# Spreading the gates of a dense expert layer from SBUF instead of DRAM, with all x tiles loaded first and a new order of streams

## The chip, the cores and the metric

One core of one Trainium2 chip runs the whole kernel. The metric is the device time of one execution in microseconds (us). Its engines are TensorE (PE, with its weight loads as PEld), VectorE (DVE), ScalarE (ACT), GpSimd (POOL) and SyncE (SP, which issues most DMAs here); sixteen DMA engines move the data. [...]

## The reference

The input is x with 8 images of 512 tokens and 128 features. Four layers are added to it one after the other, each on a layer norm of the running x:

```python
x = x + attention(layernorm(x))        # causal softmax attention, one head of 128
x = x + experts(layernorm(x))          # f = 0
x = x + rwkv_block(layernorm(x))       # a time mix with a scan over 512 tokens, and a channel mix
x = x + experts(layernorm(x))          # f = 1
```

The expert layer has 32 experts with hidden size 64. Each token takes the four experts with the highest softmax scores, and its gate for an expert is that score; an expert takes at most 2048 tokens. On top stands one shared expert of hidden size 128:

```python
y[tok] += (silu(xg @ W1[e]) * (xg @ W3[e])) @ W2[e] * gate      # for each expert e and its tokens
out = y + (silu(x @ Ws1) * (x @ Ws3)) @ Ws2
```

All is in float32.

## The kernel before, in words

**Streams.** The work is written as Python generators, each of which stands for one image or one page group and yields after every few instructions. A string `ORDER` of 2257 two-character entries says which generator goes on next. The instructions of each engine and each queue stand in exactly that order; nothing is reordered later. The streams are:

- `a0` to `a7`: `attention(b)` for image b, up to and with the routing of the first expert layer (`route`).
- `r0` to `r7`: `rwkv(b)`, up to and with the routing of the second.
- `x` and `y`: the shared expert of the first and the second expert layer.
- `s` and `t`: `scatter`, 16 indirect DMAs by which POOL writes the tokens of an image to pages of single experts in DRAM (`xs`).
- `k l m n` and `K L M N`: the four stages of `experts`, by page group: `turned` (load xg from xs, transpose), `up` (first product, acl, and gates), `down` (transposed back, hz), `give` (second product o, store of oc to `ys`). One group has up to 20 units of four pages.
- `u` and `v`: `combine`, 16 indirect DMAs that add rows of `ys` to `res`.
- `d` and `D`: `full_up`, and `e` and `E`: `full_down`, for images that use no pages.

**Two ways through the experts.** `RUNS` says that in the first layer images 0 and 7, and in the second images 6 and 7, go through all 32 experts densely, and the others through pages. Lower-case letters belong to the first layer, capitals to the second; so D6 and D7 are the two dense images at the end.

**The dense way.** `route` ends in `gates`, which makes the gate of every token and expert, transposes it to 32 partitions (one an expert) by 512 tokens, and copies it from PSUM to the SBUF tile gT (L493). That tile goes to a DRAM tile gd (L495). `full_up` then runs over 16 pairs of experts. For pair i a DMA on SP's queue fills the tile g of 128 partitions: row 2i of the gates 64 times, then row 2i+1 64 times (L692). PE multiplies the image (fT) by the pair's two weight blocks (ac, L703), ACT takes a tanh (fh, L706), and VectorE forms the activation (L709), multiplies g by the second product (L710) and both together (L711). `full_down` multiplies the result by the pair's second weights and sums over all pairs in one PSUM tile (fsum, L677), which is copied to `res` (L724) and, in the second layer, stored.

**Buffers of g.** There are four. Three loads are issued at the start of a stream, and pair i issues the load of pair i+3 ahead of its own products:

```python
        for i in range(3):
            load(i)
        yield
        for i in range(NP):
            load(i + 3)
```

The tile gT comes from the pool `work`, of which 26 buffers go round among many uses.

**The start.** SP issues, in this order: the x tiles of images 0 to 3, the clearing of the first page group's xs with zeros (two DMAs of 2.6 MB) and a strip of ys, the x tiles of images 4 to 7, and the expert weights (pair, w2s, w13s). The small weights go on ACT's queue. The clearing of the second page group follows inside `attention(0)`.

Of the kernel before, what the change touches and what calls it, by code (L numbers as in the profile page):

```python
# [79 lines left out]


ORDER = (
    "a2a0a2a1a0a2a2a0a1a3z0a2a0a1a6a3z0a0a2a3a4a2a0a1a0a6a6a4a1a2a2a5a0z0a0a2a2a1a4a5a0a0a2a5a2a0a0a2"
    "a1a3a0a3a2a7a2a0a2a0a2a1a2a2a0a3a7a0a2a1a6a3a0a0a7a2a0a2a1a2a1a0a2a1a2a2a3a0a2a1a4a3a1a2a2a0a0a1"
    "a2a0a0a3a2a0a5a1a2a2a3a2a0a0a1a1a3a2a1a1a3a0a1a2a0a7a3a0a2a0a1a2a0a3a2a0a1a3a2a6a1a0a3a1a6a0a3a6"
    "a2a1a0a3a6a2a2a0a1a0a3a2a6a2a2a0a1a6a6a0a1a3a0a1a1a0a3a0a1a6a0a1a1a0a0a3a6a3a3a1a1a3a0a6a6a1a0a0"
    "a3a1a6a2a1a3a0a6a2a3a6a4a3a4a3a4a1a1a3a4a4a1a0a5a4a4a5a1a1a3a0a6a3a1a0a3a1a6a1a4a6a3a4a4a1a3a6a1"
    "a5a3a6a3a4d0a6a5a1a3a3a6a1a1a3a2a1a4a2a5a4a4a5d0a2a1d0a5a5a2a5x0x0a2a1a2s1a3a3a6x2a4a5a6x2x0x2x2"
    "a5a6a3a4a3x2x2a6s2a4a4d0a3x2a6a3a4a6a5x0a3a4a6a5a4s2a3a6a4x0a6a3a3a4a5d0a3d0s2x0a3a6x0a7a3a6l0a6"
    "a4a7s3l0a6l0a6a4a5d0a4a5a4x3a6a4a6x3d0s3a4d0a4a5d0a7a5a5a7a5a7a4a5a7d0a6a4a5x3s3a6a4a5a4x3a5a4a5"  # L90
    "x3a4a5x3a4a5s3a5x3a5a5a7a5e0a7a5a7e0a7a5d0a4e0a5d0a7e0s2a5a6a4a5d0a5d0a6a7a6e0d0a6a7a5a7x1a5s1d0"
    "a7x1x1a4a7e0a7a4d0a4d0a4a7a4a7a7x1s1a4d0d0a7d0e0d0a7a4x1s1d0d0d0a4a4d0a7e0a4e0x1k0a5d0a6a4a5a6x1"
    "d0a5d0k0a4a5k0e0a5d0s4k0l0k0x4l0l0a5d0x4d0a5l0s4d0m0a5e0m0l0a5d0d0e0l0l0l0s4m0a5m0k0k0k0l0k0d0a5"
    "n0s4n0l0a5d0l0l0d0n0m0d0n0e0m0k0l0k0a7s5n0l0l0l0l0n0a6a7l0l0x4l0k0a6m0k0k0a6e0s5k0m0m0x5m0l0a6x5"
    "n0d0n0d0n0l0l0x5s5a6x5l0n0a7x4a7a6k0l1m0k0x5l1m0x5d0s6l1l0x5x4n0l0l0l0l0n0k0l0l0m0l0k0a7m0k0l0a7"
    "k0s6m0l0l0n0l0m0a7n0k0l0a7k0m0l0l0n0l0m0x4n0s6a7k0x4l0k0m0l0l0n0l0m0a7n0n0a7k0l0n0s6k0m0l0l0a7l0"
    "m0k0l0a7k0a7m0n0m0x6n0l0s5l0n0l0x6l0n0k0l0l0m0x6x6k0l0m0e0k0l0x6k0a7m0l0l0n0l0m0x6n0a7a7k0l0k0m0"
    "l0n0l0l0a7m0l0n0a7k0x6l0m0k0k0n0k0l0a7l0m0l0n0a7k0a7m0k0n0m0n0n0l0a7l0l0n0k1l0a7a7m0a7l0l0a7m0n0"
    "l0l0n0k1l0l0m0l0a7k1m0k1l1a7k1m0l1l1n0l1m0x7n0l1x7m1x7k1l1l1l1n0k1x7n0m1m1k1x7m1l1k1n1l1l1l1l1n1"
    "u2k1m1l1l1l1k1n1m1x7n1m1l1x7m1k1l1l1n1l1k1e7n1l1u2m1l1l1k1l1n1m1k1d0n1d0m1k1d0m1n1k1l1n1n1l1l1d7"  # L100
    "l1l1u2n1k1m1l1l1l1k1e0m1k1m1l1k1m1n1l1l1l1l1n1k1m1l1l1l1k1n1u2m1k1m1n1l1m1k1n1l1l1d0l1n1d0m1d0k1"
    "m1n1k1l1n1n1u1l1l1l1l1n1k1m1l1l1l1k1e0m1k1m1r2e0l1m1k1n1r0d7n1r2d7n1l1l1l1r0n1k1m1r2k1r0u1r0d7l1"
    "m1r0l1n1r0d7e7l1r0l1n1r2u1m1k1r0r0m1k1l1d7r0r0d7r0l1l1l1l1r0u1n1r0m1k1n1l1r2e7r2r0r2r0r0r0r0r0m1"
    "u3r0l1n1k1d7r0n1r0r2k1d7r2k1r0k1r2r0u3r0r0l1r0m1r1m1n1r0l1n1k1r1l1l1l1r0m1r1r0r1u3r2r2d7r1l1r1e7"
    "l1r0r1r0m1u3r0d7r0l1r1r0r2l1d7r1r0r2r2r2r2r0r1m1r0r0r1r1d7r0r0m1r3r1l1r0r0l1r1r3l1n1r0l1r0r1n1r3"
    "r1r1r3m1r0r0m1r1r1r1r2r1n1r0r2r3d7r0e7r0r1n1n1r1d7n1r0r0r1r0r1r0u4r0r0r1r1r0r1r0r1r2r0r1r0u4r0r0"
    "r1r2r1r0y0r1r3t0r2r1r3r2y0r1r1r3r2r3r1t0r2r1r3r1r1r3r3r2r1r1d7r3r2r1t0r3r1r3r2y0d7r1r2r1r3r3d7t0"
    "r3d7r3e7r1r1r3r3r2d7r1r2u4r3r2r1e7r2d7r3y0r2r2r2r3r2r2r1r2r2r3u4r2r2r1r2r2r3r3r1d7r3r1r3r2d7r1u5"
    "d7r1y0r2d7r1r4d7r1d7e7r4r1r2d7r3r2u5r1r4r4r1r4r1d7r2e7d7e7r4r4r1r3r2r3u5r1y1r4r4d7y1r3r4r4d7y1r3"
    "d7r3r4r2d7y1u5r4r3r4r4r4r4d7r3r4r3y1r4r4y1r3r4d7r3y1u6e7r4r3r4r3e7r3r3r4y0r3r4r3y0r5u6r4r4r2r2r3"  # L110
    "d7r3r4r4r5r2r3d7r2r3r4d7r2u6e7r5r2r5r4r2r5r2r5d7d7r4r5r3r2r2d7r2u6r4r5e7r5r4r4r2r4r5r5r5r2r4L0r3"
    "r3d7t2r4L0d7r4L0r6r5r4d7r3r5r4r4d7d7r5r6r4r4t2r3r6e7r5r5r4r4r5r5r5r5r6r5r3t2r6r5e7r4r3r4d7r5r5t2"
    "y2r4r4y2r5r5r6r3r4r6r5t1r4r5r6r6r4r3d7r6r6r4r3r3e7r4r5r4e7t1r4r6r5r5r4r5r6r5r6r4r3r6t1r4r3r5r5r6"
    "r5r4r5r5r5t1r4r5r5r5r5r5r5r6r4r4r6t4y4r5r6r5r6y4K0r6r6r5r5K0t4K0K0K0L0r6L0L0L0L0K0M0L0L0L0M0N0t4"
    "K0r6M0N0K0L0M0N0K0r6N0L0L0L0L0t4K0M0L0L0L0M0N0K0r6M0N0K0L0M0r3N0K0L0L0r7y3N0r5r6y3r5t3r5L0L0y3M0"
    "L0L0K0y4M0r5L0K0N0r5r6y2M0N0K0r6t3r5M0L0K0N0r5r5y3N0y4r5L0L0L0r6y3M0K0r5r5t3M0L0K0N0y3N0r5y2y3r7"
    "r5L0r6r5y5L0r6L0L0t5K0M0L0K0L1r7M0L1y4N0L0L1y2r7L0L0r6K0L0N0M0t5r6r7r7r6r6M0r7K0L0t5L0N0r6r7K0N0"
    "M0L0K0M0r6L0L0N0L0r6L0N0M0t5L0L0K0L0r6M0N0K0L0r6M0N0L0K0M0r6N0L0L0K0t3N0L0r6M0L0K0r6M0N0L0L0K0N0"
    "L0r6M0L0K0r6M0L0L0K0y5y5N0r6M0N0L0M0K0L0N0L0L0K0r6N0M0L0r6M0r6K0N0K0K0N0L0r6r7L0L0K0L0r7r6r7r6M0"
    "K0L0r7M0N0L0L0K0L0N0r6r7L0M0L0K1r7y5M0L0y4r6r7N0r7r7M0y4L0N0y5M0r6L0N0L0L0r6K1r7y5N0K1r6r7M0L1y5"  # L120
    "M0K1N0L1L1r6L1K1N0r7M1L1r6r6M1N1r6r7K1N1v0y2L1L1r6K1L1L1y2r6L1L1r7M1L1r6K1y6M1N1K1r7y6M1L1M1v2N1"
    "N1L1L1y6K1L1N1y6K1L1D6y6M1L1L1K1r7y6M1K1L1L1y6N1L1L1r7v2M1N1K1E6M1N1L1K1L1N1M1r7K1M1r7K1L1L1L1L1"
    "r7N1v2L1L1r7M1N1K1M1L1N1K1L1N1M1L1L1K1M1L1N1K1M1L1N1M1r7N1L1L1L1v2K1N1D6K1r7D6M1D6r7K1L1M1N1L1L1"
    "L1K1D6N1D6v0M1K1D6M1r7N1K1L1N1r7D6L1L1r7v2D6r7L1K1D6r7M1r7v0M1L1K1r7N1L1L1D6L1N1K1M1K1r7M1E6r7L1"
    "v0N1D6L1L1D6r7N1E6r7r7L1L1r7M1L1K1M1r7L1L1K1v1M1L1v0r7M1N1L1L1L1K1N1N1K1L1N1M1L1L1K1L1r7v1M1K1M1"
    "L1r7M1r7N1K1N1N1L1L1L1K1K1D6N1r7K1D6M1r7v1r7E6D6E6L1M1N1L1L1L1L1N1r7M1L1L1L1E6M1N1r7M1D6v1N1M1D6"
    "N1D6r7N1r7D6r7D6E6D6r7v4D6r7r7v1r7D6r7E6D6r7r7y7y7D6y7v4D6D6y7E6D6y7D6D6y7E6y7v4D6D6D6E7E6D6D6D6"
# [15 lines left out]
def kernel(ctx: ExitStack, tc: tile.TileContext, x, small, vecs, w13, w2, out):  # L143
    nc = tc.nc
# [536 lines left out]
    def full_up(f, b):  # L683

        n = f"{f}_{b}"
        _, gd, xT, _ = routed[f][b]
        loaded = {}

        def load(i):
            if i < NP:  # L690
# [1 line left out]
                nc.sync.dma_start(  # L692
                    out=loaded[i], in_=gd[2 * i : 2 * i + 2].unsqueeze(1).to_broadcast([2, H, S])
                )
# [319 lines left out]
```

## Time and profile before

| | us |
|---|---|
| Runs shown | median 1059.47, from 1058.66 to 1060.27 |
| The profiled execution, in all | 1047.35 |
| Its span, first to last instruction | 1045.6 |
| PE busy | 806.6 (77% of the span) |
| POOL busy | 617.1 (59%) |
| VectorE busy | 588.2 (56%) |
| ScalarE busy | 474.1 (45%) |
| g loads (L692) | 64, of 256 KB each |
| gd stores (L495) | 4, of 64 KB each |
| Data moved by DMA | 108.15 MB, 103 GB/s on average |

Busy shares are averages over stages with different limits; no engine is busy all the time. So the lines to look at are those of waits and of the chain of work that ended last. A line such as `958.40 17.41 DMA g<-gd` in the chain gives the start, the length and what was waited for. A line of the timeline gives the start, the length, the engine, the line of the kernel, the operation, what it writes and reads, their shapes, and in brackets how long the engine stood idle before it and what ended that. In a DMA view, the share of a queue is the time of its packets as a share of sixteen engines over the stretch that is asked for.

### The profile page before, as it was taken

Reading aid. Unit: us, or ns where it says so; the run is one execution under the profiler, and the core shown is the slowest. Engines: PE = TensorE matmul, PEld = TensorE weight load, DVE = VectorE, ACT = ScalarE, POOL = GpSimd, SP = SyncE. Lnnn points to the kernel's source line nnn. Section 1 sums busy time; section 2 is a strip of 40 time slices with the busy share of each in tenths; the row PEclk is TensorE's granted clock in tenths of the full one; section 3 lists DMA queues with packets and bytes.
Section 4 is the critical chain, followed back from the end, with each engine's and each line's share of the span. In section 5 each row is a group of like instructions: output and inputs, shape, how many; then the busy total and the mean of one; then the engine's idle time right before and its main releaser. Section 6 shows DMA issues by size and latency. Waiting matters only on the chain.

```text
span 1045.6 us, 14396 instructions
## 1 busy us (share of the span) xinstructions
PE 806.6 (77%) x4096; PEld 559.8 (54%) x4096; DVE 588.2 (56%) x2008; ACT 474.1 (45%) x1130; POOL 617.1 (59%) x682
## 2 busy tenths in 40 slices
PE   4488689777599668787889888786993989856664
PEld 2266356555498555453455545564783757534332
DVE  2457576655245436699779679662482445522332
ACT  4375243323276447473445555455672656201010
POOL 4200778555701828848888888878036685788500
PEclk9699999978799979898999898898996999977787
DMA  9990112333356655322233211543456566344311
GB/s 271 249 262 25 69 57 74 110 91 100 94 143 160 137 136 126 58 56 33 59 59 54 41 42 42 158 114 107 111 138 129 126 147 137 80 75 91 65 58 54
DMA packets 158892, 108.15 MB, mean 103 GB/s; under 512 B 17760, under 2 KB 147168, under 8 KB 158560
## 3 DMA queue, kind: packets, MB, share of 16 engines
q1 hardware_dynamic: 124592, 80.59, 28.8%
q0 software_dynamic: 33792, 25.39, 13.9%
q10 hardware_dynamic: 432, 1.27, 0.4%
q8 instruction: 35, 0.57, 0.2%
q14 instruction: 41, 0.34, 0.1%
HBM read 60.32 MB, written 46.89 MB: 103 GB/s over the span
## 4 chain that ended last, share of the span: by engine, by line
PE 17%; DMA 13%; POOL 11%; issue 8%; DVE 7%; ACT 2%; SPq 1%; POOLq 0%; ACTq 0%; DVEq 0%
DMA g<-gd 7%; POOL res L657 6%; DMA xg<-xs 4%; POOL xs L506 3%; PE o L609 3%; PE acl L576 3%; PE turn_x L346 1%; DMA res<-ys,rows 1%; PE kk L926 1%; PE fsum L677 1%; PE ac L703 1%; POOL idle L308 1%; PE kv L935 1%; PE acl L597 1%; DMA ys<-oc 1%
## 5 line engine op out<-in xcount | busy, mean ns | idle before, releaser
L657 POOL DMA_INDIRECT res<-ys,rows x192 | 309.2, 1610 | 123.7 <-DMA xg<-xs 57.8
L506 POOL DMA_INDIRECT xs<-xn,rows x192 | 195.7, 1019 | 83.1 <-issue 61.8
L703 PE MATMUL ac<-fT,pair 128*128 128x512 f32 x256 | 138.9, 670 | 13.1 <-DVE g L710 13.0
L706 ACT ACTIVATE fh<-ac 128x512 f32<-128x512 f32 x64 | 38.2, 596 | 162.3 <-PE ac L703 130.6
L677 PE MATMUL fsum<-w2s,fh 128*128 128x128 f32 x512 | 78.5, 305 | 39.3 <-DVE fh L711 38.9
L677 PEld LDWEIGHTS fsum<-w2s,fh 128*128 128x128 f32 x512 | 73.1, 216 | 64.7 <-DVE fh L711 52.1
L576 PE MATMUL acl<-w13s,xgTs 128*128 x640 | 94.5, 294 | 16.3 <-issue 6.1
L609 PE MATMUL o<-w2s,hz 128*128 x640 | 94.1, 292 | 15.2 <-ACT wt L585 5.8
L609 PEld LDWEIGHTS o<-w2s,hz 128*128 128x128 f32 x640 | 85.4, 203 | 28.6 <-issue 11.6
L576 PEld LDWEIGHTS acl<-w13s,xgTs 128*128 128x128 f32 x640 | 85.0, 205 | 27.4 <-issue 13.4
L710 DVE TENSOR_TENSOR g<-g,ac 128x512 f32<-128x512 f32 x64 | 43.7, 682 | 88.7 <-DMA g<-gd 88.7
L346 PE MATMUL turn_x<-ident,xg 128*128 128x128 f32 x320 | 52.8, 292 | 46.7 <-DMA xg<-xs 45.5
L703 PEld LDWEIGHTS ac<-fT,pair 128*128 128x128 f32 x256 | 50.1, 215 | 59.6 <-issue 41.2
L564 ACT COPY xgTs<-turn_x 128x512 f32<-128x512 f32 x80 | 46.7, 583 | 72.5 <-PE turn_x L346 52.8
L335 POOL TENSOR_TENSOR rstd_f<-rstd_f,nhalf 128x4 f32<-128x4 f32 x16 | 19.5, 1217 | 100.6 <-DVE wt L581 42.6
L581 DVE TENSOR_TENSOR wt<-acl,xg 128x4 f32<-128x4 f32 x80 | 12.8, 161 | 108.9 <-PE acl L576 74.6
L587 DVE SCALAR_TENSOR_TENSOR h<-h,acl 128x256 f32<-128x256 f32 x80 | 33.5, 418 | 68.0 <-ACT h L584 59.0
L346 PEld LDWEIGHTS turn_x<-ident,xg 128*128 128x128 f32 x320 | 40.6, 152 | 52.9 <-DMA xg<-xs 39.5
L615 ACT COPY oc<-o 128x512 f32<-128x512 f32 x80 | 46.8, 585 | 41.5 <-PE o L609 20.9
L602 ACT COPY hz<-acl 64x256 f32<-64x256 f32 x160 | 58.2, 364 | 13.2 <-PE acl L597 8.5
L709 DVE SCALAR_TENSOR_TENSOR fh<-fh,ac 128x512 f32<-128x512 f32 x64 | 43.6, 681 | 26.3 <-ACT fh L706 17.3
L308 POOL MEMSET idle<- 128x192 f32 x192 | 55.0, 287 | 0.0
(265 smaller groups left out, 1615.0 us busy)
## 6 DMA issues: line engine op xcount, KB each, us to landing
xg<-xs SPq DMA_DIRECT2D x80, 260.0 KB
ys<-oc SPq DMA_DIRECT2D x80, 256.0 KB
g<-gd SPq DMA_DIRECT2D x64, 256.0 KB
xs<-zero SPq DMA_DIRECT2D x4, 2600.0 KB
xs<-xn,rows POOLq DMA_INDIRECT x192
res<-ys,rows POOLq DMA_INDIRECT x192
res<-in_x_dram SPq DMA_DIRECT2D x8, 256.0 KB
pair<-in_w_dram SPq DMA_DIRECT2D x1, 2048.0 KB
```

What stands on the lines that cost most here:

```text
L308: nc.gpsimd.memset(idle, 0.0)
L346: nc.tensor.transpose(p[:, j * P : (j + 1) * P], src[:, j, :P], ident)
L506: i = nc.gpsimd.indirect_dma_start(out=xs[g][:, :], out_offset=bass.IndirectOffsetOnAxis(ap=rows[:, j, k : k + 1], axis=0), in_=xn[:, j, : ...
L564: nc.scalar.copy(xT, p)
L576: nc.tensor.matmul(acl[:, j, :EW], xT[:, j * P : (j + 1) * P], w13f[:, bass.ds(at[j], EW)], start=True, stop=True)
L602: nc.scalar.copy(z[half, i, :].rearrange("p (j c) -> p j c", c=H), hT[half])
L609: nc.tensor.matmul(o[:, j * P : (j + 1) * P], z[:, j % 2, j // 2 * P : (j // 2 + 1) * P], w2h[j % 2][:, bass.ds(at[j], P)], start=True, st ...
L615: nc.scalar.copy(flat(oc), o)
L657: nc.gpsimd.indirect_dma_start(out=xa[:, j, :], out_offset=None, in_=ys[g][:, :], in_offset=bass.IndirectOffsetOnAxis(ap=rows[:, j, k : k ...
L677: nc.tensor.matmul(p[:, j * P : (j + 1) * P], h[:, j * P : (j + 1) * P], w, start=False, stop=stop and j == NJ - 1)
L703: nc.tensor.matmul(ac[:, s, :], pair[:, i, s, :], xT, start=True, stop=True)
L710: nc.vector.tensor_tensor(v, v, ac[:, 1, :], ALU.mult)
```

## The change

The store of the gates to DRAM goes; the tile gT itself is handed on, and each g load reads its two rows from there. All eight x tiles are issued ahead of the clearing of xs. `ORDER` is replaced by another one with the same 2257 entries in other places; each stream has as many entries as before. Image 1 now comes ahead of image 0 at the start, for example, and D6's first entry is at place 1924 instead of 1882, counted from 0.

```diff
 ORDER = (
-    "a2a0a2a1a0a2a2a0a1a3z0a2a0a1a6a3z0a0a2a3a4a2a0a1a0a6a6a4a1a2a2a5a0z0a0a2a2a1a4a5a0a0a2a5a2a0a0a2"
...
+    "a1a2a2a0a1a2a2a1a0a3z0a2a1a0a6a3z0a1a2a3a4a2a1a0a1a6a6a4a0a2a2a5a1z0a1a2a2a0a4a5a1a1a2a5a2a1a1a2"
...
     "E7"
 )
@@
-    load_x(0, 4)
+    load_x(0, B)
     sm = const.tile([P, NCOLS], F32, tag="sm", name="sm")
@@
     clear(0)
-    load_x(4, B)
@@
         gT = block([E, S], name=f"gT_{n}")
         nc.scalar.copy(gT, p[:E, :])
-        gd = dram.tile([E, S], F32, tag=f"gd{n}", name=f"gd_{n}")
-        nc.sync.dma_start(out=gd, in_=gT)
-        routed[f][b] = (xa, gd, xT, None)
+        routed[f][b] = (xa, gT, xT, None)
         yield
@@
     def full_up(f, b):
...
-        _, gd, xT, _ = routed[f][b]
+        _, gT, xT, _ = routed[f][b]
...
                 nc.sync.dma_start(
-                    out=loaded[i], in_=gd[2 * i : 2 * i + 2].unsqueeze(1).to_broadcast([2, H, S])
+                    out=loaded[i], in_=gT[2 * i : 2 * i + 2].unsqueeze(1).to_broadcast([2, H, S])
                 )
```

The last rows of both orders, from D6's last entries on, show how the two dense images of the end stand to the rest:

```
before  ...D6E6v4D6D6D6D6D6E6D6D6D6D6D6v3E6D7E6D6D6E6v4D7D7D7E6v3E6D7D7D7E7D7D7D7D7E7v3...
after   ...D6D6D6r7D6D6r7r7D6D6D6r7v3E6r7E6D6D6r7v4E6r7D7y7D7y7y7D7y7v3E6y7D7y7E6D7y7D7D7E7E7D7v5...
```

More of the change, by code (lines that the diff above doesn't have):

```diff
@@ L82 @@
 ORDER = (
-    "a2a0a2a1a0a2a2a0a1a3z0a2a0a1a6a3z0a0a2a3a4a2a0a1a0a6a6a4a1a2a2a5a0z0a0a2a2a1a4a5a0a0a2a5a2a0a0a2"
[L84 to L127, printed above, removed]
@@ L128 @@
-    "E6v4D6D6D6D6D6E6D6D6D6D6D6v3E6D7E6D6D6E6v4D7D7D7E6v3E6D7D7D7E7D7D7D7E7v3D7D7D7E7D7D7v3D7E7D7D7D7"
-    "E7D7v5D7D7E7v3D7D7D7E7v5D7D7D7E7D7D7D7E7v5D7D7D7E7D7D7D7E7v5D7D7D7D7D7E7D7D7D7D7D7E7E7v5D7D7E7E7"
+    "a1a2a2a0a1a2a2a1a0a3z0a2a1a0a6a3z0a1a2a3a4a2a1a0a1a6a6a4a0a2a2a5a1z0a1a2a2a0a4a5a1a1a2a5a2a1a1a2"
+    "a0a3a1a3a2a7a2a1a2a1a2a0a2a2a1a3a7a1a2a0a6a3a1a1a7a2a1a2a0a2a0a1a2a0a2a2a3a1a2a0a4a3a0a2a2a1a1a0"
+    "a2a1a1a3a2a1a5a0a2a2a3a2a1a1a0a0a3a2a0a0a3a1a0a2a1a7a3a1a2a1a0a2a1a3a2a1a0a3a2a6a0a1a3a0a6a1a3a6"
@@ new lines @@
+    "a2a0a1a3a6a2a2a1a0a1a3a2a6a2a2a1a0a6a6a1a0a3a1a0a0a1a3a1a0a6a1a0a0a1a1a3a6a3a3a0a0a3a3a6a0a3a6a0"
+    "a6a0a3a6a0a3a6a0a3a4a3a4a4a0a3a3a6a4a0a0a6a3a4a6a3a0a6a0a3a0a3a3a4a0a0a6a4a6a6a4a3a0a3a3a6a6a0a1"
+    "a0a2a3a6a0a3a2a4a5a1a6a1a2a5a3a2a1a3a6a3a6a6a2a1a3a5a5a1a5a2a5s1a5a7a5a5a7a7a2a0a7a2a0a3s2a0x2d0"
+    "d0x2a6x2d0x2a4a3a4a5x2a5d0s2x2a3a3a6x2a4a5a4d0a5a3d0a4a5s2x0x0a3a6a3a6l0l0a4l0a6a5s3a4a6a5x0a6a4"
+    "a4a5x3a6a5a4a6a4x0x3a4a5s3a4a5a4x3a5a4x3a4a5a5x3a4x0x3a4a5a6a5d0a4x3s3a5x0a6a4a5a4x0a5a4d0a4a5s3"
@@ new lines @@
+    "d0a4a5d0a4a4a5d0a4a5a4a7s2a5a7a7a5x1a6a5a6a5a7a6a5a7e0a4x1a6e0s1a4a7e0d0x1a4e0d0x1a7a4x1d0a4a5d0"
+    "a4d0a7s1a4e0a7a7x1a4d0x1a4a5d0a7d0s1d0a4a4d0a7e0a4e0a6d0a4k0a5a6d0d0a5a4x4a5k0d0x4s4e0k0k0l0k0x4"
+    "a5a7d0a5l0l0a5d0x4a7a7s4a5l0a7d0k0a5m0k0e0m0l0a5n0s4d0n0l0l0a5d0a6a7a6l0a5e0s4m0a6m0l0l0l0a6k0k0"
+    "n0l0a6n0k0m0a6k0m0a5x5s6l1l0x5d0l0l0l0l0e0l0l0l0m0m0s6d0x5x4d0k0d0l1k0m0k0m0l0k0l1a7x5l0l0l0l0s6"
+    "k0l0l0x5x5k0l0k0x5n0k0m0n0n0m0m0s6x4n0m0l0x4n0l0l0l0l0n0k0l0l0n0l0s5k0m0n0n0m0k0n0m0l0k0m0n0l0l0"
@@ new lines @@
+    "d0l0n0d0s5k0d0m0k0n0m0a7l0n0a7n0l0l0l0l0a7n0k0l0l0m0s5l0a7k0x6m0k0l0a7k0m0x6l0n0l0x6m0a7l0n0l0a7"
+    "s5k0l0l0m0l0n0k0m0a7n0k0a7l0k0m0l0l0n0l0m0x6n0l0a7x6k0l0l0m0l0n0k0m0a7k0n0l0k0m0a7k0l0l0n0k0l0a7"
+    "m0n0k0a7l0a7m0k0n0m0l0x6a7l0l0n0l0k1x6a7m0a7l0n0e0l0a7l0m0e0l0n0a7k1l0l0m0l0n0k1m0a7k1n0l1k1m0a7"
+    "l1l1n0a7m0n0n0d0n0l1d0k1m1d0k1m1l1a7u2l1l1l1m1k1a7a7m1l1k1n1l1l1l1l1a7n1k1m1l1l1l1k1n1m1e0u2n1m1"
+    "a7k1m1l1k1n1l1l1l1l1n1k1m1l1l1l1k1n1m1a7n1m1k1m1l1u2k1n1l1l1l1l1a7n1k1m1l1l1l1k1n1m1x7n1m1k1m1l1"
@@ new lines @@
+    "k1n1l1l1u2l1l1x7n1k1m1l1l1l1k1n1m1k1m1n1x7l1m1k1n1l1l1d0l1n1d0m1u1d0k1m1n1k1l1n1r2d0d0l1l1n1d0x7"
+    "n1d0l1d7d0r2k1m1d0k1e0m1u1e0l1r2r2x7d7l1l1r2l1n1x7r2m1k1d7u1m1d7e0k1l1n1r2x7l1l1l1e0l1r2r0m1k1m1"
+    "r2k1l1l1r0l1l1r2k1l1l1m1r0u1l1n1m1r0e7m1r2r2k1n1r0k1r0l1e7l1m1r0u3k1l1l1k1r2r0r0k1r1m1r0k1l1r0r0"
+    "r2k1l1l1l1r1r2n1r0n1n1u3m1m1r0r0l1r0r0r2r0l1r0r0l1n1n1r0m1d7n1r0u3r0d7n1r0n1n1n1r0r0r0u3l1r0m1r1"
+    "r0m1r1n1l1r2r1l1r1d7r0l1d7r0l1r2r0r1r3r2m1r0m1e7r0r2r3r1r1d7r0n1r0r1r1r2r1r0r2r2r0r1n1r0r1r0r2r1"
@@ new lines @@
+    "r0r0r0r0r3r2r0r0r1r1r3r2r2r0r1n1r1r1r0r2r1r1r3r0r1u4r0r1r1r0r1r1u4r0r0r3r2r0d7r0r3r1r1r0r3r3r0r0"
+    "r1r2d7r3r1u4d7r2r3r0r1d7r2r1r3r1r0r0d7r3r0d7r2u4e7r0r1r1r0e7r1r2r3r1d7r3y0r1r1d7r1r2t0r1r3r3d7r2"
+    "r1r4r3r1r2r2y0r1d7e7r4r1r2y0t0r3r4r4r3r3r4r2r4r1d7r3r3r2r4t0r3d7r1r4r3r4r3r1t0r1r2r4r3r2r4d7r4r3"
+    "r1r3r2r4d7u5r2r4r1r2d7r4d7r4r1r4r1r4d7r2r4r4r1r3r1r2u5r4r1r4r4e7r2e7r4d7e7y0r4u6r4r4r1r4r1r4r2r1"
+    "r4r4u5r4r1r4r4r1r4r4r4r1r2r4r3r3r1u6y1r2d7r4r4y0y1d7r4y1r4r2y1r3r4y1e7u5r3r4y1r4r3d7r4y1d7r2u6r4"
@@ new lines @@
+    "r4r2r5r2r4r3r4r2d7r3r2d7r4r3r5r2r4r3d7r4u6r3r5r4r5d7r4e7r4r2r2r2r3r5r3e7r5t1r4r5r6r3r2r3d7r4r5r5"
+    "r3r6r2r3r5L0r5t2r6r6d7L0r5r3L0r3r5r5t2r5r5r5r5r5r5r6d7r5r5e7r3r5t2d7y0r5y2y0y2r5r5t2r5r3r5r5r6r6"
+    "r5d7d7r3r6r5d7r3t1r5r6y2d7r5r3d7r5r3e7r5r3r5r6t1d7r6r3d7r5r5r3r6r5r3r5r6t1d7r5r3r6r6r6r6d7r6d7r5"
+    "r6r3e7r5r5r3r4r5K0r3r5r4r4r3K0r4e7K0K0L0K0e7y2r4L0r5L0r5r4e7t4L0r3M0K0r5r6L0M0N0K0L0L0r5y3N0y4t4"
+    "y3L0L0y4K0M0L0L0L0M0K0N0y3r6M0N0K0L0M0t4r6N0K0L0L0r6y3N0L0L0K0M0L0L0L0M0t4K0M0y3N0M0r6L0N0N0L0L0"
@@ new lines @@
+    "r6K0N0K0y3L0r5L0y3r5t3r5r6M0K0r6L0r7M0L0K0L0N0r6L0N0r6t3M0K0M0r5L0L0y4K0N0L0r5L0N0y2M0L0L0K0L0r5"
+    "M0r6y4K0N0r5r6t3r5r6M0L0K0N0r6L0M0r6r5y4L0r6K0N0r5t3L0L0N0K0M0L0L0L0K0r6M0r5N0r6M0N0L0r7M0K0L0N0"
+    "L0r5K0r6N0y4r6L0L0r5y4K0M0L0L0r5r6M0L1N0t5L0K0L1r6L0L1N0M0r7L0K0M0r6L0N0L0K0L0N0r6M0L0K0t5r6M0y5"
+    "L0N0L0K0r6L0N0M0L0K0M0r6L0t5L0K0r7N0y5r6M0N0L0y5M0K0L0N0L0t5L0K0K0N0L0K0M0L0L0r6M0L0N0r6M0L0r6N0"
+    "M0K0N0K0K1L0r6L0r7L0L0y5L0M0r6r7y5y5N0M0N0L0L0K1r6r7N0M0K1K1M0L1K1N0L1L1L1L1N0r7K1L1L1M1L1K1r6r7"
@@ new lines @@
+    "M1r6y5M1L1v0r7r7M1N1L1L1L1K1N1N1K1L1N1M1L1L1K1L1r6M1r7K1r6r6M1L1v0r7M1N1L1L1L1K1N1N1K1L1N1r6r7L1"
+    "L1L1r7M1K1r6M1M1r6v0y2M1K1r6L1r6r7y2N1L1L1r7K1N1N1L1K1L1N1r7K1M1L1L1r6M1L1v0N1K1L1r6N1M1r7r7K1L1"
+    "M1y6r7L1D6N1L1K1D6N1y6D6r7M1K1M1y6y6K1D6v2L1N1L1L1L1L1N1K1M1L1L1L1M1v0N1K1y6M1L1N1r7M1K1N1v1K1L1"
+    "L1y6r7N1L1L1y6K1M1L1L1r7E6M1N1K1D6L1N1D6v2K1D6M1K1E6M1L1r7N1D6L1L1L1N1D6K1M1D6K1r7M1v1L1r7N1r7D6"
+    "N1L1L1L1D6E6K1M1D6K1E6M1L1r7N1L1L1r7v2L1L1r7K1L1M1r7L1E6L1M1N1D6K1r7M1N1D6r7M1K1L1N1D6v1K1N1K1N1"
@@ L130 @@
+    "L1D6L1L1K1D6r7D6L1r7M1L1L1r7v2L1M1E6r7L1M1L1L1N1L1M1r7N1N1r7M1D6M1N1N1D6v1D6r7N1E6r7r7v2D6r7D6r7"
+    "D6v4D6r7v1D6D6r7D6r7r7v4E6E6D6D6E6D6D6D6E6r7v4D6r7r7E6D6r7D6r7r7r7D6r7D6E6v4D6D6D6r7D6D6r7r7D6D6"
+    "D6r7v3E6r7E6D6D6r7v4E6r7D7y7D7y7y7D7y7v3E6y7D7y7E6D7y7D7D7E7E7D7v5D7D7E7D7D7D7E7v3D7D7D7E7D7D7D7"
+    "E7v5D7D7D7E7D7D7D7E7v3D7D7D7E7D7D7D7E7v5D7v3D7D7E7D7D7v5D7E7D7D7D7D7D7E7D7D7D7D7D7v5E7E7D7D7E7E7"
     "E7"
```

## The prediction

> **What bounds the kernel now.** I read the page first: its chain of work that ended last, then the groups.
>
> ```profile
> DMA g<-gd 7%; POOL res L657 6%; DMA xg<-xs 4%; POOL xs L506 3%; PE o L609 3%; PE acl L576 3%; PE turn_x L346 1%; DMA res<-ys,rows 1%; PE kk L926 1%; PE fsum L677 1%; PE ac L703 1%; POOL idle L308 1%; PE kv L935 1%; PE acl L597 1%; DMA ys<-oc 1%
> ...
> L710 DVE TENSOR_TENSOR g<-g,ac 128x512 f32<-128x512 f32 x64 | 43.7, 682 | 88.7 <-DMA g<-gd 88.7
> ```
>
> The largest single entry of the chain is the load that the change edits, and VectorE's idle time before L710 is all put down to it. The chain of the last stretch says where it lies, and the timeline of VectorE with what rhythm:
>
> ```profile
> 958.40 17.41 DMA g<-gd
> ...
> 978.93 37.70 DMA g<-gd x2
> ...
> 1018.24 19.78 DMA g<-gd
> ```
>
> ```profile
> 1022.00 0.69 DVE L710 TENSOR_TENSOR g<-g,ac 128x512 f32<-128x512 f32 x1 [3.33 <-DMA g<-gd]
> ...
> 1027.35 0.69 DVE L710 TENSOR_TENSOR g<-g,ac 128x512 f32<-128x512 f32 x1 [3.34 <-DMA g<-gd]
> ...
> 1032.69 0.69 DVE L710 TENSOR_TENSOR g<-g,ac 128x512 f32<-128x512 f32 x1 [3.34 <-DMA g<-gd]
> ...
> 1038.04 0.69 DVE L710 TENSOR_TENSOR g<-g,ac 128x512 f32<-128x512 f32 x1 [3.34 <-DMA g<-gd]
> ```
>
> One pair of experts every 5.35 us, whatever the engines do (PE is busy 18.7 of the 33 us from 1005): from about 900 us on, the rate of the g loads is the rate of the kernel. Next, what one load occupies, and what a read from SBUF by the same kind of packet costs. The DMA view of a stretch with hardly anything but g loads, then of the 0.55 us in which gd is stored from gT with nothing else on the queue:
>
> ```profile
> DMA packets 161, 0.27 MB, mean 50 GB/s; under 512 B 2, under 2 KB 40, under 8 KB 161
> ...
> q1 hardware_dynamic: 161, 0.27, 13.3%
> ```
>
> ```profile
> DMA packets 48, 0.07 MB, mean 119 GB/s; under 512 B 16, under 2 KB 16, under 8 KB 48
> ...
> q1 hardware_dynamic: 48, 0.07, 49.1%
> ```
>
> First: 13.3% of 16 engines is 2.1 engines. A load is 128 packets of 2 KB on two engines, 64 each, so 5.35 / 64 = 84 ns a packet. Second: 49.1% of 16 x 0.55 us is 4.32 us; less 16 completion marks of about 9 ns, 4.2 us over 32 packets of the same 2 KB: 131 ns, with single packets up to 162 ns. The SBUF side is the slow one here.
>
> Last, the start, where VectorE stands still for a late x tile (the seventh entry of its order works on image 6):
>
> ```profile
> 32.80 0.87 DVE L314 BATCH_NORM_STATS2 stats_a<-res 128x6 f32<-128x128 f32 x4 [16.88 <-DMA res<-in_x_dram]
> ```
>
> [...] an xg load issued behind three g loads took 18.30 us (below).
>
> **The change, part by part.**
>
> *The source of g.* [...] From the trace: 5.35 x 131/84 = 8.3 us at least [...], 5.35 x 162/84 = 10.3 us at most. I take 9.7. From below, if two readers don't disturb each other, it remains 5.35, since an engine's own rate (84 ns) sets that; nothing speaks for less.
>
> *The gd stores.* Four go, with 0.34 us of SP's issue and about 2 us of landing each. The wait for gT does not go: it moves to the first g load, on the same queue, with xg and ys behind it. Worth 0 to 2 us; I take 0. gT now holds a buffer of `work` (26) through its stage; fT is held as long already. I take 0, up to 10 us.
>
> *All x tiles first.* Four tiles (1 MB) at the 250 to 271 GB/s of these windows are 4 us, so image 6 is there at about 15 us instead of 32.8, and the clearing of xs, 4 us later, is not needed before the first scatter at 97.7. The weights land no later: the bytes of the first 78 us, in which the DMA is full, are the same. At most 16.9 us, at least 5 (if DMA fullness hands it back); I take 15.
>
> *The order.* It holds the same 2257 entries. What counts is where the last two whole images start. I count places from 0. D6's first loads stand at 1882 before, at 1924 after. At 1924 seven units of the last page (N1) have been given; before, the seventh stands at 1934. SP's timeline and the chain:
>
> ```profile
> 783.44 7.45 SPq L692 DMA_DIRECT2D g<-gd  x3
> ...
> 819.11 0.36 SPq L616 DMA_DIRECT2D ys<-oc  x1
> ```
>
> ```profile
> 790.98 18.30 DMA xg<-xs
> ```
>
> The seventh unit's store is at 819; less the 18 us, which the three g loads ahead of that xg caused and which now come later, 801. Less 15 from the start, 786. Before that point d0 and d7 pass. d0's first product now stands 13 places after its loads, some 6 us at half a microsecond a place (d0's products at places 360 and 601 run at 144.9 and 257.5 us), so VectorE waits some 6 us. d7's three first loads hold the queue 3 x 4.35 = 13 us longer, with two units of prefetch as cover. The other loads of d0 stand 8 or 9 us apart, near their price. For both I take 7 (0 to 25): D6's first load at 793.
>
> From there all 32 loads of images 6 and 7 run one behind the other. Each pair issues the load of three pairs later, so two or more always wait; the experts' places between D6's first pair and N1's end are 25 a pair, some 11 us, which about equals one load. The hand-over to D7 is covered: r7's last gate product stands before D6's last pair, so gT7 is copied while that pair's load is in flight. Sum: 793 + 2 (first landing) + 32 x 9.7 (310) + c + 8 (from the last landing to the end; now 1038.0 to 1045.6). c is what else these two engines carry on the same queue: 13 ys and 7 xg units at 0.9 us (32 packets of 28 ns) and six image stores, 23 us if nothing overlaps. The gathers are on another queue: now 8 loads beside them take 55 us instead of 43[...]. I take 20 (5 to 45). The span becomes 1133 us against 1045.6: +87. The profiled execution took 1047.35 in all, 1.75 round its span; the runs shown have a median of 1059.47, 12 more. 1059.5 + 87 = 1147 us.
>
> POOL's gathers end at about 985 now and have 140 us to spare then; PE, 57% busy from 1005 to 1038, is no bound either.
>
> **The rivals.**
>
> *The read from SBUF is not slowed (0.14).* For it: the slow packets of the gd store might be slow for their target in DRAM, written by 16 engines at once; in the later stores, which queue behind other traffic, many packets took 84 to 96 ns. Against: [...] a stretch at 250 GB/s or more of clearing shows that DRAM takes more than this store wrote. Then loads stay at 5.35, the rhythm of the end stays, and about the start's gain remains: 1045 us (1030 to 1062). This is the case on the other side. It decides below 6.96 us a load: 793 + 2 + 32 x 6.96 + 20 + 8 is the present span.
>
> [...] At 10.3 us a load, and xg and ys stuck behind g loads on the same rings with VectorE waiting in order, the experts of the last page end 25 us later and nothing overlaps: 793 + 25 + 2 + 330 + 45 + 8 = 1203, 1217 us as a run.
>
> *Slower loads, yet covered (0.05).* If image 6's loads hid wholly under the last page's experts, only image 7's would count: 16 x 4.35 = 70, less 15: 1115 us. Against: at N1's end (2103) only seven of its 16 pairs are through by the order.
>
> **How the numbers follow.** My forecast, 1147, has 0.74. Its own range, from the ends of D6's start (784 to 821), the load (9.3 to 10.3) and c, not all high at once, is 1110 to 1205; [...] I widen it to 1085 to 1205, leaving out the first rival and half the second. About 2% can be told from no change by a measurement of this kernel. Slower by over that: 0.74 + 0.07 + 0.05 = 0.86, less 0.01 for a mild mixture. The first rival's 0.14 straddles the bound: 0.09 within, 0.05 faster; the mixture goes within, 0.10.
>
> **What would show it.** Right: VectorE's L710 lines in the last 100 us 9 to 10 us apart; its idle time for g well over 200 us in total; g's stretch still about 2 engines busy, at half the GB/s; no 16.9 us gap before L314. [...] the start step if another idle time of that length follows; the sum, if the D6 loads begin outside 784 to 821 us.

## The result, and the profile after

The changed kernel takes 1222.41 us in the median (1220.88 to 1223.95) against 1059.47: a ratio of 1.154, with an interval of 1.147 to 1.161. The prediction, 1147 us with a range of 1085 to 1205, has the direction and misses the size by 75 us. The profiled execution took 1223.95 us, its span 1222.2; before, 1047.35 and 1045.6. So the spans differ by 177 us where the prediction had 87.

The page's chain of work that ended last, and its two groups of most interest (line, engine and tiles, count, busy time and mean ns, then the idle time ahead and what ended it):

```profile
DMA g<-gT 17%; POOL res L654 9%; DMA xg<-xs 8%; PE acl L573 4%; PE o L606 4%; DMA res<-ys,rows 3%; PE turn_x L345 2%; PE ac L700 2%; SPq L689 2%; PE o L776 1%; DMA ys<-oc 1%; SPq L613 1%; PE fsum L674 1%; PE s L756 1%
...
L707 DVE TENSOR_TENSOR g<-g,ac 128x512 f32<-128x512 f32 x64 | 43.7, 683 | 173.5 <-DMA g<-gT 164.9
...
L345 PE MATMUL turn_x<-ident,xg 128*128 128x128 f32 x320 | 56.7, 307 | 113.0 <-DMA xg<-xs 110.3
```

The g load has 17% of the chain instead of 7%, and VectorE waits 164.9 us for it instead of 88.7. But there are new names as well: xg, the page tile of the other way through the experts, has 8% instead of 4%, and SP's own issue of g loads (SPq L689) has 2%. PE stood idle 110.3 us for xg; before, the list of waits has 45.5 us for the same.

The end, as the chain of waits tells it, and the timeline of VectorE in the last 50 us:

```profile
1028.18 34.84 DMA g<-gT
...
1067.31 124.25 DMA g<-gT x5
...
1191.89 22.46 DMA g<-gT
```

```profile
1164.93 0.69 DVE L707 TENSOR_TENSOR g<-g,ac 128x512 f32<-128x512 f32 x1 [3.75 <-DMA g<-gT]
...
1175.18 0.69 DVE L707 TENSOR_TENSOR g<-g,ac 128x512 f32<-128x512 f32 x1 [8.24 <-DMA g<-gT]
...
1180.76 0.69 DVE L707 TENSOR_TENSOR g<-g,ac 128x512 f32<-128x512 f32 x1 [3.57 <-DMA g<-gT]
...
1191.59 0.69 DVE L707 TENSOR_TENSOR g<-g,ac 128x512 f32<-128x512 f32 x1 [8.81 <-DMA g<-gT]
```

Near the end the pairs now come about 10 and 6 us apart in turn. From D7's first gate product at 1083.78 to the last at 1214.38 there are 15 intervals, 8.7 us each; before, the same 15 intervals take 6.1 us each, and the last ones 5.35. The packets of the loads show where the time goes. In a stretch with one g load by itself beside POOL's gathers (on the other queue) the DMA view gives:

```profile
DMA packets 669, 0.51 MB, mean 43 GB/s; under 512 B 61, under 2 KB 541, under 8 KB 669
...
q1 hardware_dynamic: 129, 0.26, 10.9%
```

The second line is the load: 10.9% of 16 engines over the 11.7 us asked for is 20.4 us, over 128 packets of 2 KB 159 ns each (the median over all packets of the kernel's g loads is 152), where one from gd took 84. Two engines are still at work; each is nearly half as fast. The slowing is not constant: in D7 the packets come in stretches near 150 and stretches near 84 ns (47% of them are below 100 ns, and 25% in D6), which is the rhythm of 10 and 6 us. What switches it off was not tested.

What the prediction did not see coming lies earlier. SP's timeline around the first dense image, before and after (start, length from the first to the last of the issues that are drawn together, time between them included, and their number):

```profile
92.30 94.54 SPq L692 DMA_DIRECT2D g<-gd  x12
189.04 0.94 SPq L554 DMA_DIRECT2D xg<-xs  x2
```

```profile
100.63 80.54 SPq L689 DMA_DIRECT2D g<-gT  x10
181.26 22.54 SPq L551 DMA_DIRECT2D xg<-xs  x2
```

Two xg loads, which SP issues in 0.94 us in the kernel before, now hold it for 22.54 us (17.03 and 5.46 by themselves). This is read as a queue that stays full while the g loads ahead of them are not through. Summed issue by issue over the first expert layer, SP stands in them for 90 us for g, 89 for xg and 33 for ys; before, 29, 28 and 21. D6's first load, the point from which the prediction counted the end, is issued at 871.8 us; before at 783.4:

```profile
871.84 9.88 SPq L689 DMA_DIRECT2D g<-gT  x3
```

So 88 of the 177 us are lost before that point and 88 after it (350 to the end instead of 262).

### The profile page after: what moved, and what is told of

It reads as the page before. It is cut to its first block, busy times and chain, and to the rows that moved or that the text cites. A ratio compares the mean times of both kernels' runs of the same rounds, so it can differ in the third digit from the quotient of the medians.

```text
span 1222.2 us, 14375 instructions
## 1 busy us (share of the span) xinstructions
PE 834.5 (68%) x4096; PEld 583.4 (48%) x4096; DVE 588.0 (48%) x2008; ACT 474.6 (39%) x1130; POOL 612.3 (50%) x682
## 4 chain that ended last, share of the span: by engine, by line
DMA 30%; PE 28%; issue 13%; POOL 11%; DVE 9%; ACT 3%; SPq 3%; another core or an unknown queue 2%; POOLq 0%; ACTq 0%; DVEq 0%
DMA g<-gT 17%; POOL res L654 9%; DMA xg<-xs 8%; PE acl L573 4%; PE o L606 4%; DMA res<-ys,rows 3%; PE turn_x L345 2%; PE ac L700 2%; SPq L689 2%; PE o L776 1%; DMA ys<-oc 1%; SPq L613 1%; PE fsum L674 1%; PE s L756 1%
## 5 line engine op out<-in xcount | busy, mean ns | idle before, releaser
L654 POOL DMA_INDIRECT res<-ys,rows x192 | 306.1, 1594 | 192.4 <-issue 48.8
L674 PE MATMUL fsum<-w2s,fh 128*128 128x128 f32 x512 | 82.6, 318 | 76.9 <-DVE fh L708 76.8
L345 PE MATMUL turn_x<-ident,xg 128*128 128x128 f32 x320 | 56.7, 307 | 113.0 <-DMA xg<-xs 110.3
L707 DVE TENSOR_TENSOR g<-g,ac 128x512 f32<-128x512 f32 x64 | 43.7, 683 | 173.5 <-DMA g<-gT 164.9
L674 PEld LDWEIGHTS fsum<-w2s,fh 128*128 128x128 f32 x512 | 76.8, 229 | 99.1 <-DVE fh L708 91.1
L573 PE MATMUL acl<-w13s,xgTs 128*128 x640 | 96.4, 298 | 22.4 <-DVE g L707 10.9
L606 PE MATMUL o<-w2s,hz 128*128 x640 | 96.6, 299 | 15.3 <-issue 4.8
L703 ACT ACTIVATE fh<-ac 128x512 f32<-128x512 f32 x64 | 38.1, 595 | 172.7 <-PE ac L700 139.0
L345 PEld LDWEIGHTS turn_x<-ident,xg 128*128 128x128 f32 x320 | 43.9, 161 | 122.5 <-issue 78.2
L606 PEld LDWEIGHTS o<-w2s,hz 128*128 128x128 f32 x640 | 89.1, 212 | 27.0 <-issue 12.1
L581 ACT ACTIVATE h<-acl 128x256 f32<-128x256 f32 x80 | 30.7, 384 | 60.2 <-DVE wt L578 52.4
```

What stands on the lines that cost most here:

```text
L345: nc.tensor.transpose(p[:, j * P : (j + 1) * P], src[:, j, :P], ident)
L573: nc.tensor.matmul(acl[:, j, :EW], xT[:, j * P : (j + 1) * P], w13f[:, bass.ds(at[j], EW)], start=True, stop=True)
L606: nc.tensor.matmul(o[:, j * P : (j + 1) * P], z[:, j % 2, j // 2 * P : (j // 2 + 1) * P], w2h[j % 2][:, bass.ds(at[j], P)], start=True, st ...
L654: nc.gpsimd.indirect_dma_start(out=xa[:, j, :], out_offset=None, in_=ys[g][:, :], in_offset=bass.IndirectOffsetOnAxis(ap=rows[:, j, k : k ...
L674: nc.tensor.matmul(p[:, j * P : (j + 1) * P], h[:, j * P : (j + 1) * P], w, start=False, stop=stop and j == NJ - 1)
L707: nc.vector.tensor_tensor(v, v, ac[:, 1, :], ALU.mult)
```

## The experiments

Each result is a ratio to the kernel before on the same chip. Chips differ: in the first batch (e1, e2, e4, e5) the kernel before takes 999 us, in all others 1058 to 1062. So ratios are compared, and places in us only where the kernel before takes about 1060. The expectations of the first batch are in us for such a chip; in that measure e1 comes to 1269 us, above its range, and e2, e4 and e5 to 1023, 1019 and 940, below theirs. "Term (4)" below is the prediction's 7 us for the dense images of the first layer, "the sum from D6" its 340 us after D6's first load.

### Source or order?

**e1**: only the source of g is changed, in the kernel before.

```diff
-        gd = dram.tile([E, S], F32, tag=f"gd{n}", name=f"gd_{n}")
-        nc.sync.dma_start(out=gd, in_=gT)
-        routed[f][b] = (xa, gd, xT, None)
+        routed[f][b] = (xa, gT, xT, None)
```

> The kernel before with one edit alone: g is read from gT in SBUF; old order, old start. Theory ([...] xg and ys wait behind those loads on the same queue): nearly the whole loss is here, 1200 to 1235 us, packets of g about 150 ns, a load 9 to 11.5 us. Rival (the source accounts for the end alone, some 85 us, and the new order for D6's late start): 1130 to 1155 us.

**e2**: the opposite edit in the changed kernel, so that new order and early x tiles remain, and g comes from gd.

> The changed kernel with one edit taken back: g is read from gd in DRAM again; new order and all x tiles first are kept. Theory: the start's gain is left over, D6's first load near 770 us, 1030 to 1060 us. Rival (the new order is itself at fault): 1100 to 1135 us, with D6's first load still past 840 us.

Measured: e1 1204.82 us, ratio 1.198 (1.190 to 1.207); e2 964.05 us, 0.966 (0.960 to 0.972). The whole loss is the source, and more than the whole: what surrounds it gains 3.4%, and 1.154 / 0.966 = 1.195 lies within e1's interval. Gate packets in e2 take 84 ns again.

**e3**: only the x tiles are moved, in the kernel before.

```diff
-    load_x(0, 4)
+    load_x(0, B)
...
-    load_x(4, B)
```

> The kernel before with one edit alone: all eight x tiles are issued ahead of the clearing of xs; old order, gates from DRAM. Theory: the 16 us that VectorE stood still for image 6 stay gained to the end, 0.982 to 0.990 of the time before, and the other half of what order and start gained together (0.966) is the order's. Rival (the gain of the start is taken up by later waits): 0.995 to 1.005.

Measured: 1048.83 against 1061.34 us, 0.989 (0.985 to 0.993). The wait of 16.9 us for image 6 is gone; what arrives at the end is 12.5 us of it. The share of the order by itself was not separated on one chip; 3.4% and 1.1% leave about 2% for it.

### Why is the load slow?

**e4**: the gate product is written in another order of columns, so that the two rows of pair i lie 16 partitions apart in gT. As many packets, engines and bytes, from the same tile.

```diff
-        nc.vector.tensor_tensor(gate, gate, ex, ALU.mult)
+        nc.vector.tensor_tensor(
+            gp.rearrange("p j (two n) -> p j n two", two=2), ..., ALU.mult)    # gate, ex: n, two swapped
...
-            nc.tensor.transpose(p[:E, j * P : (j + 1) * P], gate[:, j, :], ident)
+            nc.tensor.transpose(p[:E, j * P : (j + 1) * P], gp[:, j, :], ident)
...
-                    out=loaded[i], in_=gT[2 * i : 2 * i + 2].unsqueeze(1)...
+                    out=loaded[i], in_=gT[i : i + NP + 1 : NP].unsqueeze(1)...
```

> The changed kernel with the gates of a pair on partitions i and 16+i of gT instead of 2i and 2i+1, by writing the last gate product in another order of columns; still SBUF, still two engines a load. [...] Theory: packets of g go back to about 84 ns, a load to 5.4 us, and the time to that of the changed order with DRAM, 1030 to 1060 us. Rival (a read from SBUF by one engine is slow by itself, wherever the other reads): packets stay at 150 ns and the time at 1222 us.

Measured: 961.27 us, 0.962 (0.958 to 0.966), the same as e2's load from DRAM. Packets take 84 ns in the median, and the timeline of VectorE near the end has the rhythm of before:

```profile
934.50 0.69 DVE L711 TENSOR_TENSOR g<-g,ac 128x512 f32<-128x512 f32 x1 [3.34 <-DMA g<-gT]
...
939.85 0.69 DVE L711 TENSOR_TENSOR g<-g,ac 128x512 f32<-128x512 f32 x1 [3.33 <-DMA g<-gT]
...
945.19 0.69 DVE L711 TENSOR_TENSOR g<-g,ac 128x512 f32<-128x512 f32 x1 [3.33 <-DMA g<-gT]
```

So SBUF as a source is not slow (84 ns a packet); two neighbouring rows read at the same time are (152 in the changed kernel). Only distances of 1 and 16 partitions were tried.

**e6**: the changed kernel with each load as two DMAs of one row, which spreads each over 16 engines (in the trace below 89.9% of all 16 are busy).

```diff
-                nc.sync.dma_start(
-                    out=loaded[i], in_=gT[2 * i : 2 * i + 2].unsqueeze(1).to_broadcast([2, H, S])
-                )
+                for s in range(2):
+                    nc.sync.dma_start(
+                        out=loaded[i][s * H : (s + 1) * H],
+                        in_=gT[2 * i + s : 2 * i + s + 1].unsqueeze(1).to_broadcast([1, H, S]),
+                    )
```

> The changed kernel with each g load as two DMAs of 64 partitions from one row of gT each, so that sixteen engines share it[...]. Theory [...] a packet of g takes above 0.5 us on its engine, and the time stays at 1.12 to 1.22 of before, since xg and ys now meet those packets on every engine. Rival (an engine's own reading of SBUF is the limit): loads go eight times as fast, 0.86 to 0.90.

Measured: 1211.61 us, 1.140 (1.134 to 1.147). The DMA view of 20 us near the end:

```profile
DMA packets 379, 0.62 MB, mean 31 GB/s; under 512 B 74, under 2 KB 74, under 8 KB 379
...
q1 hardware_dynamic: 379, 0.62, 89.9%
```

Here 89.9% of 16 engines are busy, yet all together move 31 GB/s: 305 packets of 2 KB take 0.94 us each. Eight times the engines give nearly the same time, so what limits the load is shared. It lies on the side of the rows that are read, for e8 writes the same destinations from DRAM in the same way, and its packets take 84 ns in the median. With two engines it was 2 x 2048 B / 152 ns = 27 GB/s.

### What costs 92 us in the first layer?

**e7**: the changed kernel, with the first layer's gates through gd again and the second layer's from gT.

```diff
-        routed[f][b] = (xa, gT, xT, None)
+        if f == 0:
+            gd = dram.tile([E, S], F32, tag=f"gd{n}", name=f"gd_{n}")
+            nc.sync.dma_start(out=gd, in_=gT)
+            routed[f][b] = (xa, gd, xT, None)
+        else:
+            routed[f][b] = (xa, gT, xT, None)
```

> The changed kernel with gates from DRAM in the first expert layer (d0, d7) and from SBUF in the second (D6, D7). Theory (both layers lose: d0 and d7 by late xg units behind their loads, D6 and D7 by the pace of the end): about half of the loss comes back, 1.04 to 1.08 of before. Rival (the loss is all at the end, and what the first layer loses is covered): 1.13 to 1.16. Other rival (it is nearly all in the first layer): 0.97 to 1.01.

Measured: 1141.39 us, 1.078 (1.072 to 1.083). D6's first load is at 780.2 instead of 871.8, and from there to the end it takes 348 us instead of 350. PE's waits for xg fall to less than half:

```profile
780.18 9.32 SPq L694 DMA_DIRECT2D g<-gT  x3
```

```profile
PE turn_x L345 <- DMA xg<-xs: 51.0, 8, 27.9
```

(total us, times, longest.) The place in SP's timeline that was shown above, and beside it e9's, where g still comes from gT (its experiment is the next):

```profile
102.20 69.32 SPq L694 DMA_DIRECT2D g<-gd  x10
173.00 0.93 SPq L556 DMA_DIRECT2D xg<-xs  x2
```

```profile
100.20 81.26 SPq L691 DMA_DIRECT2D g<-gT  x10
181.50 23.75 SPq L553 DMA_DIRECT2D xg<-xs  x2
```

So the slow load in the first layer alone costs 92 us between these two profiled executions, for which term (4) had 7. That of e7 was the fastest of its four; by the ratios, 1.154 less 1.078 of 1059 us, it is about 81 us. In what way it costs this, the next runs ask.

**e9**: the loads are issued as before, but VectorE multiplies by a constant tile instead of g, so it never waits for a load there. The gates are left out of the dense images' sums.

```diff
-            v = loaded.pop(i)
...
-            nc.vector.tensor_tensor(v, v, ac[:, 1, :], ALU.mult)
+            v = full.tile([P, S], F32, tag="gv", name=f"gv_{n}_{i}", bufs=2)
+            nc.vector.tensor_tensor(v, gconst, ac[:, 1, :], ALU.mult)
```

> The changed kernel, but VectorE multiplies by a constant tile instead of g, so that nothing waits for the loads (the gates are left out of the product of the dense images); all g loads are still issued at the same places. Open is how the first layer loses 92 us. Theory (xg and ys wait behind g loads on the same rings): most of it remains, D6's first load at 835 to 875 us on a chip where the kernel before takes 1060, and the whole is 1.07 to 1.12 of before, since the loads must still drain. Rival (VectorE, in order, waits for g and holds up all else): D6's first load at 770 to 800 us and 1.00 to 1.05.

**e12**: the changed kernel as it is, on the same chip as e9 and e10.

> The changed kernel unaltered, as the measure for the two runs above on the same chip: 1.14 to 1.16, PE's wait for xg near 110 us, D6's first load near 870 us where the kernel before takes 1060.

Measured: e12 1228.04 us, 1.161 (1.153 to 1.170), D6's first load at 873.2. e9 1259.34 us, 1.186 (1.179 to 1.193), D6's first load at 914.7. Both expectations for e9 are missed, upwards. The waits of e9:

```profile
PE turn_x L347 <- DMA xg<-xs: 124.7, 9, 37.0
...
DVE e L861 <- DMA g<-gT: 71.4, 1, 71.4
```

PE's waits for xg are there without VectorE waiting for g at its product, so VectorE's order is not needed to make them. In the changed kernel VectorE waits 10 us for g in the whole first layer, which leaves that rival little. How large the waits would be otherwise e9 does not tell: freed of VectorE, SP runs ahead into the full queue, and its issues for g take 196 us in the first layer instead of 86 in e12. The second line is a single wait of 71.4 us for the g loads elsewhere: L861 writes a tile e1 of the pool `work`, the pool of gT, so its buffer is most likely one that loads still read. That wait is new in this kernel, and how it makes e9 slower than e12 was not pursued.

**e10**: the g loads are issued from ScalarE's queue, so that xg and ys are alone on SP's.

```diff
-                nc.sync.dma_start(
+                nc.scalar.dma_start(
```

> The changed kernel with the g loads issued from ScalarE's queue, so that xg and ys no longer stand behind them in one ring; [...] ScalarE now stands still while its queue is full. Theory (the queue): PE's wait for xg before L345 falls from 110 to under 60 us, D6's first load comes at 790 to 835 us, and the whole is 1.07 to 1.13. Rival [...]: the xg wait stays near 110 us and the whole at 1.14 to 1.18.

Measured: 1225.41 us, 1.156 (1.150 to 1.163). The waits:

```profile
ACT fh L703 <- issue: 89.5, 11, 14.0
...
ACT hs L525 <- issue: 49.5, 4, 26.6
...
PE turn_x L345 <- DMA xg<-xs: 46.3, 11, 9.3
```

PE's waits for xg fall from 108.5 us (e12) to 46.3, about what they were before the change, so these waits go with the queue. But the standing moves to ScalarE, whose next instructions (fh, hs) now lie behind its issues for g, and D6's first load comes at 854.9, only 18 us earlier. Place and total miss the expectation, and the total is that of the rival, in which something other than the order of the queue delays xg. So this run speaks for the queue as the source of the waits, and does not show what they cost.

**e14**: gT gets two buffers of its own, so that it holds none of `work`.

```diff
-        gT = block([E, S], name=f"gT_{n}")
+        gT = rt.tile([E, S], F32, tag="gT", name=f"gT_{n}", bufs=2)
```

> The changed kernel with gT in buffers of its own instead of one of the 26 of the work pool, so that its longer life takes nothing from others. Theory (the held buffer costs nothing, as the prediction took it): 1.14 to 1.165, as the changed kernel. Rival (part of the first layer's loss is waits for that buffer): 1.08 to 1.13.

Measured: 1220.51 us, 1.151 (1.142 to 1.161), D6's first load at 866.9. The held buffer costs nothing that can be told.

**e13**: e7, with each first-layer load issued twice, the second into a tile that nobody reads. Its loads come from DRAM at 84 ns a packet in the median; queue and engines are to be held about as long as by slow ones, with no read from gT. In the rival it is the slow read itself that disturbs other transfers.

```diff
             if i < NP:
+                if f == 0:
+                    twice = full.tile([P, S], F32, tag="twice", name=f"twice_{n}_{i}", bufs=2)
+                    nc.sync.dma_start(
+                        out=twice, in_=gT[2 * i : 2 * i + 2].unsqueeze(1).to_broadcast([2, H, S])
+                    )
```

(gT is here the name in `full_up` of whatever `routed` holds, gd in the first layer.)

> As the run with gates from DRAM in the first layer and from SBUF in the second (1.078), but each load of the first layer is issued twice, the extra one into a tile that nobody reads. The two engines and the queue are then occupied as long as by one slow read from SBUF (2 x 5.35 = 10.7 us)[...]. Theory (the first layer loses by the time that its loads hold the ring and SP, with xg and ys behind them): the time of the changed kernel comes back, 1.13 to 1.18, D6's first load at 850 to 890 us where the kernel before takes 1060. Rival [...]: 1.075 to 1.10.

Measured: 1214.37 us, 1.149 (1.139 to 1.159). D6's first load is at 854.6, and the wait is back:

```profile
PE turn_x L345 <- DMA xg<-xs: 119.3, 10, 36.6
```

SP stands for 98 us in issues for g and another 95 in those for `twice`, 62 for xg and 44 for ys in the first layer; e7 has 38, 33 and 17, the changed kernel 90, 89 and 33. So 74 us (854.6 less 780.2) come back without a single slow read in the first layer, and the ratio is 1.149 where e7 has 1.078 and the changed kernel 1.154. As a measure of the queue this is not clean. The dose is higher: the packets of the first layer's loads take some 730 us in sum, against 635 in the changed kernel and some 370 in e7. And a doubled load holds the engines as well as the queue, which e13 does not separate. The course differs too: PE's first product with the 37th xg unit starts at 385.8 us in e7, 446.5 in the changed kernel and 457.2 in e13, so e13 has lost 71 us by then and 3 more up to D6, the changed kernel 61 and 31. Those last 31 us were not attributed. As for the engines, POOL's scatters use the same engines from another queue. In the trace of the changed kernel 14 of the 16 engines report the last scatter of the first page group by 173.5 us and the last two at 178.6 and 178.8; in e7 the 14 do by 170.2, the two at 172.7 and 173.0. What such delays cost was not separated.

### Versions that are faster than both

**e5**: the kernel before with e6's edit on gd: two DMAs of one row each.

```diff
+                for s in range(2):
+                    nc.sync.dma_start(
+                        out=loaded[i][s * H : (s + 1) * H],
+                        in_=gd[2 * i + s : 2 * i + s + 1].to_broadcast([H, S]),
+                    )
```

> The kernel before with each g load issued as two DMAs of 64 partitions, each from one row of gd; [...] sixteen engines can share a load. Theory (the pace of the end is the two engines): a load takes about 1 us plus its latency, VectorE's wait for g falls from 88.7 to under 20 us, the last 16 pairs go at 3 to 4 us each, 990 to 1015 us. Rival (the pace is set by reading one row of DRAM, or by what else is in the queue, and 64 more issues come on top): 1055 to 1090 us.

**e8**: e5's load in the changed kernel (new order, x tiles first). **e11**: e5's load and the early x tiles in the order of before.

> New order and x first, with gates from DRAM in two DMAs of 64 partitions each. Theory: the gain of order and start (0.966) and that of the sixteen engines (0.887) act in different stretches and add, 0.85 to 0.87. Rival (the order's gain was a better cover for slow g loads, which are gone): 0.88 to 0.895.

> The fastest parts together: the old order, all x tiles first, g from DRAM in two DMAs of 64 partitions each. Theory (both gains are in different stretches and add): 0.989 x 0.887 = 0.877, 0.870 to 0.885. Rival (once the end is fast, another wait, such as the gathers or the scatters on GpSimd, takes back the start's gain): 0.887 to 0.895.

Measured: e5 885.66 us, 0.887 (0.883 to 0.891); e8 948.92 us, 0.894 (0.890 to 0.899); e11 946.49 us, 0.891 (0.886 to 0.895). The gains expected to add up (0.85 to 0.87 and 0.877) did not; both runs came out where their rivals had them. The three are not told apart: with a fast load, neither order nor early x tiles add anything that can be measured. The waits of e5, SP's timeline near the end and SP's queue in the DMA view of 10 us there show that the bound has moved:

```profile
DVE g L712 <- DMA g<-gd: 8.6, 1, 8.6
```

```profile
850.89 8.96 SPq L693 DMA_DIRECT2D g<-gd  x12
```

```profile
q1 hardware_dynamic: 1322, 1.57, 55.9%
```

One wait of 8.6 us is left of 88.7, and SP gets through the twelve issues of six pairs in 8.96 us. With two gate rows a DMA, two engines were at work (2.1 by the trace of before, 13.3% of sixteen); with one row a DMA the queue keeps 55.9% of sixteen busy, where two could give 12.5%. e5's 11% is what that is worth in this kernel, without touching where the gates lie.

## Why the prediction was wrong

**The load (step of the source): right.** Two engines and a slower read by both were predicted, at 9.7 us, the author's estimate between the 8.3 and 10.3 us that the packets of the gd store give. The packets of the second layer's 32 loads occupy each of the two engines for 278 us, 8.7 us a load: 9.6 in D6, close to the prediction, and 7.8 in D7, where the slowing comes and goes. The sign of 9 to 10 us between pairs was not met in that form. Why the read is slow stands on the runs alone: with two engines a packet takes 152 ns from neighbouring rows and 84 from rows 16 partitions apart (e4), and sixteen engines together move 31 GB/s where two move 27 (e6). What it is that the readers share was not shown. The rival with no slowing (1045 us) fell with the first timeline.

**The start (15 us): right.** The first scatter is issued at 94.73 us instead of 107.79, 13 us earlier (the 97.7 of the prediction was POOL's work just ahead of it), and no gap of 16.9 us is left. e3, which does this part alone, gains 12.5 us.

**The sum from D6 (340 us): right within 10, in part by luck.** It took 350 (e7: 348). But the loads fill 278 us of it instead of 310, and the other 72 stand against 30 in the prediction (2 to the first landing, 20 for other traffic, 8 after the last): two errors of 32 and 42 us that nearly cancel. Loads in single file are most of the end, but not all of it: D6's 16 pairs took 195.5 us from its first load to D7's. What the 72 us are was not taken apart.

**D6's start: this is the step that failed.** "For both I take 7 (0 to 25)" was its term for d0 and d7. Without slow loads in the first layer D6 begins at 780.2 (e7), where the prediction has 786 without that term; with them at 871.8. The term is 92 us in the profiled executions (about 81 by the ratios), and its upper bound 25 was not one. Of the error of 89 us in the span, +85 is this term, +10 the sum from D6 and -6 the place of D6 without it.

Why it was missed: the prediction priced d0 and d7 by who waits for a gate, VectorE some 6 us (it waited 10 in the first layer), and by d7's first three loads, 13 us. It noted that the other loads of d0 stand about as far apart as the new price, and put them at nothing. What the runs show in that place is SP standing in its issues: two for xg take 22.54 us instead of 0.94, and the xg and ys issues of the first layer 122 instead of 49. By the reading above, loads that stand 8 to 9 us apart keep the queue full once each takes that long, and what SP issues behind them is late. How the 92 us divide between this queue, the engines that other queues share and the later part under d7 stays open (e10, e13). The list of waits before already had it, in a small way (45.5 us of PE for xg). The text even quoted an xg load that took 18.3 us behind three g loads, and used it only to move one store. The rival of 1217 us, with xg and ys stuck behind the g loads, named that mechanism, but placed it in the last page group of the second layer and gave it 25 us; by luck of its other terms its total is near the result. Its place was wrong: the cost lies in the first layer (e7), under the pages that all later images wait for.

**The sign test "well over 200 us" of idle time for g: wrong.** It was 164.9, of which 155 lie in the second layer (154 in e7). So the loss in the first layer hardly shows under g (10 us). Why the end shows no more than this was not pursued.

**The gT buffer and gd stores at 0: right** for the buffer by e14; the stores were not tried by themselves.
